# Dilated attention, then a binary convolution: group-norm statistics of two layers through one set of products

## The chip, the cores and the metric

The kernel runs on one core of one Trainium2 chip. The metric is device time in microseconds (us); the time of a kernel is the median of its runs. Profiles come from one profiled execution, whose own time is given beside its span. In the rows, PE is the matmul engine (TensorE), PEld its weight loads, DVE is VectorE, ACT is ScalarE, POOL is GpSimd and SP is the engine that issues most DMAs.

## The reference

The input `x` has 16 images of 56 x 56 pixels and 384 channels, in float32. Two layers follow each other, both with a group norm in front and a residual around them:

```python
def _gn(v, G=32, eps=1e-5):          # 32 groups of 12 channels, over a whole image
    g = v.reshape(B_, H_, W_, G, C_ // G)
    m = jnp.mean(g, axis=(1, 2, 4), keepdims=True)
    s = jnp.var(g, axis=(1, 2, 4), keepdims=True)
    return ((g - m) / jnp.sqrt(s + eps)).reshape(v.shape)

x = x + attention(_gn(x), w_qkv, w_proj, b_proj)   # layer 0
x = x + depthwise_conv3x3(_gn(x), sign(w))         # layer 1
```

The attention of layer 0 splits the channels into three sets of 128 with dilations 1, 2 and 3, each with four heads of 32 channels. Every pixel attends to its 3 x 3 neighbours at that dilation; a 384 x 384 projection with a bias follows. What matters here is that a group norm needs the mean and variance over the whole image before any pixel of it can be normalised.

## The kernel before

The work is cut into chunks of 8 rows (448 pixels): 7 chunks an image, 112 in all, numbered `m`; `b` is the image and `c` the chunk within it. Every tile has channels on the partitions, three tiles of 128.

Three stages run at once on different chunks.

- Stage A (`plan_a`) loads a chunk of `x` (L407), turns it with 12 TensorE transposes (L412), copies the three results out of PSUM on ScalarE (L424), takes their per-channel statistics on VectorE (`bn_stats`, L425) and stores them channel-first in DRAM as `xd` (L427, three stores). `xd` has three buffers, one image each. For image 0 it runs ahead of everything else.
- Stage B (`plan_b`) loads from `xd` (L455), normalises on ScalarE (L459), forms q, k and v on TensorE (L463), copies k and v out (L473) with halo rows exchanged by DMA (L477, L478), multiplies q by the shifted keys on VectorE (L516), sums over channels on TensorE (L501), takes the softmax, spreads the weights on TensorE (`pb_a`, L582), multiplies by the shifted values (L589), adds up on GpSimd (L597 to L601), projects (`po`, L615), adds the residual (L618), takes layer 1's statistics (L621) and stores `x1d` (L623).
- Stage C (`plan_c`) loads `x1d` (L694, L745), normalises (L713, L756), convolves two channel sets on TensorE (`pc`, L727) and the third on ScalarE and GpSimd (L778, L784 to L792), turns the result back (L799), copies it out (L801) and stores it.

The order of the work is a plan in slices. `at(when, order, piece)` puts a piece of work at slice `when`; nine slices make a step (`STEP = 9`), and chunk `m` of stage B starts at step `m`. All pieces are emitted in the order of slice and then of kind, and the framework makes each engine's in-order queue from that, by its own estimate of when things are ready:

```python
plan_a(m, STEP * (m - 9))
plan_b(m, STEP * m)
plan_c(m, STEP * (m + 10))
```

So before the change stage A of a chunk runs nine steps ahead of its stage B, and stage C ten steps behind.

The statistics of an image (`group_norm`) are a chain of six pieces, put at slices 0, 1, 2, 4, 5 and 7 from their start. `channels` merges the seven chunks' statistics per channel (`bn_aggr`, L305). `mean` sums channels into the 32 groups with three TensorE products (`pm`, L311). `deviation` sends the mean back to the channels (`pb`, L321) and squares the difference on GpSimd (L324, L325). `variance` sums again (`pv`, L331), `invert` takes the inverse root in 13 GpSimd operations (L345 to L349), and `spread_out` sends mean and scale to the channels (`pp`, L354, copied to `mr` at L358). For layer 1, 24 more small products (`pz`, L367) make a second copy, `mrz`, in stage C's layout. Each float32 product is two matmul instructions in the profile.

The chain runs 32 times: for layer 0 of image `b` from slice 5 of the step in which stage A has its last chunk (step 7b-3), and for layer 1 of image `b` from the start of step 7b+9. Within the seven steps of an image, numbered from 0, layer 1's chain therefore lies in the third step and layer 0's, for the image after next, in the fifth and sixth. Stage C's new image starts in the fourth.

The PSUM tiles of stage A, of k and v, of `po`, of `pc`, of the outputs and of the statistics all share one pool of three buffers, `ps_mt`.

Of the kernel before, what the change touches and what calls it, by code (L numbers as in the profile page):

```python
# [8 lines left out]
F32 = mybir.dt.float32  # L9
# [3 lines left out]
ALU = mybir.AluOpType  # L13
# [4 lines left out]
P = 128  # L18
HEADS = 4
HD = 32  # L20
NG = 3
NTAP = 9
NQ = 4
ROWS = 8
SUB = 112
GN_CH = 12
GN_G = 32
# [8 lines left out]
def dilated_attention_then_binary_conv(  # L36
# [28 lines left out]
    nc = tc.nc  # L65
    B, H, W, C = x.shape
    PX = ROWS * W
    NCH = H // ROWS
# [4 lines left out]
    K3 = 3 * HD  # L73
    JG = NG - 1
# [217 lines left out]
            for m in matmuls[1:]:  # L292
                tc.keep_in_program_order(m())

    def group_norm(stats, done, for_convolution=False):

        had = {}  # L300

        def channels():
            had["ch"] = ch = st_p.tile([P, NG, 2], F32, tag="ch", name="ch")
            for j in range(NG):
                nc.vector.bn_aggr(ch[:, j, :], stats[:, j].rearrange("p c s -> p (c s)"))  # L305

        def mean():
            had["pair"] = pair = st_p.tile([GN_G, 3], F32, tag="pair", name="pair")
            pm = ps_mt.tile([P, 512], F32, tag="mt", name="pm")
            for j in range(NG):  # L310
                nc.tensor.matmul(  # L311
                    pm[:GN_G, 0:1], gsel[:, j], had["ch"][:, j, 0:1], start=(j == 0), stop=(j == NG - 1)
                )
            nc.vector.tensor_scalar_mul(pair[:, 2:3], pm[:GN_G, 0:1], -1.0 / GN_CH)

        def deviation():

            ch = had["ch"]
            pb = ps_mt.tile([P, 512], F32, tag="mt", name="pb")
            for j in range(NG):  # L320
                nc.tensor.matmul(pb[:, j : j + 1], gselT[:, j], had["pair"][:, 2:3], start=True, stop=True)  # L321
            had["dev"] = dev = st_p.tile([P, NG], F32, tag="dev", name="dev")
            nc.vector.tensor_tensor(dev, pb[:, :NG], ch[:, :, 0], ALU.add)
            nc.gpsimd.tensor_tensor(dev, dev, dev, ALU.mult)  # L324
            nc.gpsimd.tensor_tensor(dev, dev, ch[:, :, 1], ALU.add)  # L325

        def variance():
            dev = had["dev"]
            pv = ps_mt.tile([P, 512], F32, tag="mt", name="pv")
            for j in range(NG):  # L330
                nc.tensor.matmul(pv[:GN_G, 0:1], gsel[:, j], dev[:, j : j + 1], start=(j == 0), stop=(j == NG - 1))  # L331
            had["var"] = var = st_p.tile([GN_G, 3], F32, tag="var", name="var")
            v, r = var[:, 0:1], var[:, 1:2]
            nc.vector.tensor_scalar(v, pv[:GN_G, 0:1], 1.0 / GN_CH, 1e-5, op0=ALU.mult, op1=ALU.add)

            ri = r.bitcast(I32)
            nc.vector.tensor_single_scalar(ri, v.bitcast(I32), 1, op=ALU.arith_shift_right)
            nc.vector.tensor_scalar(ri, ri, -1, RSQRT_BITS, op0=ALU.mult, op1=ALU.add)

        def invert():  # L340

            var, pair = had["var"], had["pair"]
            v, r, t = var[:, 0:1], var[:, 1:2], var[:, 2:3]
            for step in range(3):
                nc.gpsimd.tensor_tensor(t, r, r, ALU.mult)  # L345
                nc.gpsimd.tensor_tensor(t, t, v, ALU.mult)
                nc.gpsimd.tensor_scalar(t, t, -0.5, 1.5, op0=ALU.mult, op1=ALU.add)
                nc.gpsimd.tensor_tensor(pair[:, 1:2] if step == 2 else r, r, t, ALU.mult)
            nc.gpsimd.tensor_tensor(pair[:, 0:1], pair[:, 2:3], pair[:, 1:2], ALU.mult)  # L349

        def spread_out():
            pp = ps_mt.tile([P, 512], F32, tag="mt", name="pp")
            for j in range(NG):
                nc.tensor.matmul(  # L354
                    pp[:, 2 * j : 2 * j + 2], gselT[:, j], had["pair"][:, 0:2], start=True, stop=True
                )
            mr = st_p.tile([P, NG, 2], F32, tag="mr", name="mr", bufs=4)
            nc.vector.tensor_copy(mr.rearrange("p j s -> p (j s)"), pp[:, : 2 * NG])  # L358
            if not for_convolution:
                done(mr)  # L360
                return

            pz = ps_mt.tile([P, 512], F32, tag="mt", name="pz")
            for s in range(JG * NQ):
                of_set = gselT[:, s // NQ, s % NQ * HD : s % NQ * HD + HD]
                for ky in range(3):
                    nc.tensor.matmul(  # L367
                        pz[ky * HD : (ky + 1) * HD, 2 * s : 2 * s + 2], of_set, had["pair"][:, 0:2],
                        start=True, stop=True,
                    )  # L370
            mrz = st_p.tile([K3, JG, NQ, 2], F32, tag="mrz", name="mrz")
            nc.vector.tensor_copy(mrz.rearrange("p j q s -> p (j q s)"), pz[:K3, : 2 * JG * NQ])
            done(mr, mrz)

        return channels, mean, deviation, variance, invert, spread_out

# [5 lines left out]
    def at(when, order, piece):  # L382

        pieces.setdefault((when, order), []).append(piece)
# [6 lines left out]
    def plan_a(m, t0):  # L391

        b, c = divmod(m, NCH)
        had = {}

        def load():
            if c == 0:
                stats0[b] = st_p.tile([P, NG, NCH, 6], F32, tag="stats0", name="stats0")
                xd[b] = dr_p.tile([C, H * W], F32, tag="xd", name="xd")
            if b == 0 and c % 3:  # L400

                xin = z_p.tile([P, NQ * PX], F32, tag="z", name="xin_z")[:SUB, : NSUB * C]
                xin = xin.rearrange("p (s c) -> p s c", s=NSUB)
            else:
                xin = xin_p.tile([SUB, NSUB, C], F32, tag="xin", name="xin")
            had["xin"] = xin
            nc.sync.dma_start(xin, xf[b, c * PX : (c + 1) * PX, :].rearrange("(s p) c -> p s c", p=SUB))  # L407

        def turn(j):
            pt = ps_mt.tile([P, 512], F32, tag="mt", name="pt_x")  # L410
            for s in range(NSUB):
                nc.tensor.transpose(  # L412
                    pt[:, s * SUB : (s + 1) * SUB], had["xin"][:, s, j * P : (j + 1) * P], ident[:SUB, :SUB]
                )
            if b == 0:

                if j == 0:
                    pool, tag = ((xn_p, "xn"), (xn_p, "xn"), (xn_p, "xn"), (xr_p, "xr"), (t_p, "t"), (w_p, "w"),
                                 (w_p, "w"))[c]
                    first[c] = pool.tile([P, NG, PX], F32, tag=tag, name="x_first")  # L420
                xa = first[c][:, j]
            else:
                xa = xa_p.tile([P, PX], F32, tag="xa", name="xa")
            nc.scalar.copy(xa, pt[:, :PX])  # L424
            nc.vector.bn_stats(stats0[b][:, j, c, :], xa)  # L425
            if b:
# [4 lines left out]
        steps = {}  # L431

        def norm(k):
            if k == 0:
                steps["of"] = group_norm(stats0.pop(b), lambda mr: mr0.update({b: mr}))
            steps["of"][k]()

        at(t0 - 3 if b else FIRST + 2 * max(c - 2, 0), LOADS, load)
        for j in range(NG):
            at(t0 + 2 * j if b else FIRST + 2 * c + 1, STAGE_A, lambda j=j: turn(j))  # L440
        if c == NCH - 1:
            for k in range(6):
                at(t0 + 5 + STAT0_SLICE[k], STAT_ORDER[k], lambda k=k: norm(k))

    def plan_b(m, t0):

        b, c = divmod(m, NCH)
        had = {}
# [173 lines left out]
            if j == NG - 1:  # L622
                nc.sync.dma_start(chunk_of(x1d[b], c), xr)  # L623

        steps = {}

        def norm(k):
            if k == 0:
                steps["of"] = group_norm(stats1.pop(b), lambda mr, mrz: mr1.update({b: (mr, mrz)}), True)
            steps["of"][k]()  # L630
# [17 lines left out]
        at(t0 + 20, LOADS, load_residual)  # L648
        for j in range(NG):
            at(t0 + 24 + j, PROJECT, lambda j=j: out_project(j))  # L650
        if c == NCH - 1:
            for k in range(6):
                at(t0 + 27 + STAT1_SLICE[k], STAT_ORDER[k], lambda k=k: norm(k))

    def plan_c(m, t0):

# [181 lines left out]

    STAT_ORDER = (STATISTICS, SPREAD, SPREAD, SPREAD, STATISTICS, SPREAD)
    STEP = 9  # L840
    STAT0_SLICE = (0, 1, 2, 4, 5, 7)
    STAT1_SLICE = (0, 1, 2, 4, 5, 7)
    FIRST = -200
    at(FIRST, LOADS, load_weights)
    for cc in range(NG):
# [3 lines left out]
    for o in range(NTAP):  # L849
        at(-17 + o, LOADS, lambda o=o: load_taps(*divmod(o, 3)))  # L850
    at(5, LOADS, small_weights)
    for m in range(N):
        plan_a(m, STEP * (m - 9))
        plan_b(m, STEP * m)
        plan_c(m, STEP * (m + 10))
    for key in sorted(pieces):
# [30 lines left out]
```

## Time and profile before

| | us |
|---|---|
| median of 3 runs | 5411.35 |
| lowest and highest | 5409.35, 5414.15 |
| profiled execution, own time | 5406.89 |
| its span in the trace | 5405.2 |
| TensorE busy | 5205.9 |
| GpSimd busy | 4215.2 |
| VectorE busy | 4150.0 |
| ScalarE busy | 2397.8 |

The page gives busy times over the whole span. Since the work repeats every seven steps, the stretches of single steps say more than the averages; the prediction reads those. An answer for a line of the kernel gives how long its instructions were busy, the mean of one in ns, and how long its engine idled just before them and what ended that.

### The profile page before, as it was taken

The page shows a single profiled execution, that of the slowest core. Times are in us where ns is not written, and L with a number is a line of the kernel's source. Part 1 is how long each engine was busy: PE and PEld are TensorE (multiplying, and loading weights), DVE is VectorE, ACT ScalarE, POOL GpSimd, SP SyncE. Part 2 cuts the span into 40 slices and gives each one's busy share as a digit, 9 for nine tenths or more (in the row PEclk, how much of TensorE's full clock was granted, in tenths as well). Part 3 has the DMA queues.
Part 4 walks back from the last instruction along what each step waited for, and adds up shares of the span by engine and source line. Part 5 has one row for each costly group of instructions (what it writes and reads, how often), then busy time and mean ns, then how long its engine had stood idle before and what let it go on. Part 6 is the DMA issues. An engine that isn't in the chain of part 4 may idle for free. (4 is left out here: it accounts for less than half of the span.)

```text
span 5405.2 us, 77297 instructions
## 1 busy us (share of the span) xinstructions
PE 5205.9 (96%) x27669; PEld 2414.4 (45%) x27669; DVE 4150.0 (77%) x4209; ACT 2397.8 (44%) x4189; POOL 4215.2 (78%) x3049
## 2 busy tenths in 40 slices
PE   8999999999999999999999999999999999999965
PEld 4444444444444444444444444444444444444422
DVE  4887777878777787777777777787777778777754
ACT  3224444444444444444444444444444444444433
POOL 2677888888888887888888788888888888888880
PEclk9999999999999999999999999999999999999976
DMA  5444555655555555555655655555555655544443
GB/s 168 127 120 124 159 157 158 163 154 161 158 158 160 164 159 159 157 157 158 163 154 161 164 152 160 164 157 163 159 157 154 164 154 161 161 130 134 122 130 126
DMA packets 810799, 825.73 MB, mean 153 GB/s; under 512 B 359467, under 2 KB 800174, under 8 KB 810414
## 3 DMA queue, kind: packets, MB, share of 16 engines
q1 hardware_dynamic: 802430, 808.79, 54.2%
q10 hardware_dynamic: 7984, 12.00, 0.7%
q8 instruction: 219, 3.59, 0.3%
q14 instruction: 166, 1.36, 0.1%
HBM read 466.41 MB, written 231.21 MB: 129 GB/s over the span
## 5 line engine op out<-in xcount | busy, mean ns | idle before, releaser
L597 POOL TENSOR_TENSOR w<-w 128x1344 f32<-128x1344 f32 x672 | 2049.9, 3050 | 456.2 <-DVE w L589 396.7
L589 DVE TENSOR_TENSOR w<-pb_a,v 128x1344 f32<-128x1344 f32 x1008 | 1559.1, 1547 | 267.0 <-PE pb_a L582 177.4
L516 DVE TENSOR_TENSOR t<-pq,k 128x1344 f32<-128x1344 f32 x1008 | 1535.8, 1549 | 237.0 <-PE pq L463 236.1
L463 PE MATMUL pkv<-xn,wqkvT 128*128 128x448 f32 x3924 | 1569.9, 549 | 9.0 <-ACT xa L424 4.7
L463 PEld LDWEIGHTS pkv<-xn,wqkvT 128*128 128x128 f32 x3924 | 718.4, 190 | 671.8 <-issue 629.4
L615 PE MATMUL po<-y,wprojT 128*128 128x448 f32 x2016 | 834.9, 550 | 27.4 <-POOL y L601 15.0
L784 POOL TENSOR_TENSOR m<-m 128x1344 f32<-128x1344 f32 x210 | 644.7, 3070 | 274.1 <-ACT m L778 274.0
L463 PE MATMUL pq<-xn,wqkvT 128*128 128x448 f32 x1962 | 830.7, 558 | 0.0
L713 ACT ACTIVATE z<-z,mrz 96x448 f32<-96x448 f32 x840 | 578.3, 751 | 350.9 <-DMA z<-x1d 330.3
L501 PE MATMUL ps<-t,sel 128*32 128x448 f32 x6048 | 666.0, 550 | 26.0 <-DVE t L516 25.3
L778 ACT ACTIVATE m<-zg,ktap 128x448 f32<-128x448 f32 x945 | 555.5, 658 | 274.0 <-POOL m L784 266.9
L615 PEld LDWEIGHTS po<-y,wprojT 128*128 128x128 f32 x2016 | 376.4, 191 | 382.9 <-issue 341.1
L727 PE MATMUL pc<-z,kdiag 96*32 96x440 f32 (+1 forms) x5040 | 516.7, 543 | 6.4 <-POOL z L715 4.6
L463 PEld LDWEIGHTS pq<-xn,wqkvT 128*128 128x128 f32 x1962 | 344.0, 189 | 316.9 <-issue 316.9
L734 DVE TENSOR_TENSOR x<-pc,x 128x448 f32<-128x448 f32 x224 | 139.3, 622 | 353.2 <-PE pc L727 342.1
L582 PE MATMUL pb_a<-aT,spread 24*128 24x448 bf16 x3024 | 369.1, 359 | 32.2 <-DVE w L589 25.9
L601 POOL TENSOR_TENSOR y<-y,w 128x448 f32<-128x448 f32 x336 | 381.5, 1135 | 22.6
L618 DVE SCALAR_TENSOR_TENSOR xr<-po,bias,xr 128x448 f32<-128x448 f32 x336 | 227.5, 677 | 220.9 <-PE po L615 217.2
L600 POOL TENSOR_TENSOR y<-w 128x448 f32<-128x448 f32 x336 | 382.2, 1138 | 14.7
L473 ACT COPY v<-pkv 128x448 f32<-128x448 f32 x336 | 178.3, 531 | 484.1 <-PE pkv L463 475.8
L473 ACT COPY k<-pkv 128x448 f32<-128x448 f32 x336 | 178.2, 530 | 376.5 <-PE pkv L463 376.5
L501 PEld LDWEIGHTS ps<-t,sel 128*32 128x32 f32 x6048 | 170.6, 110 | 364.9 <-issue 247.8
(131 smaller groups left out, 4394.7 us busy)
## 6 DMA issues: line engine op xcount, KB each, us to landing
z<-x1d SPq DMA_DIRECT2D x570, 224.0 KB
xr<-xd SPq DMA_DIRECT2D x112, 672.0 KB
x1d<-xr SPq DMA_DIRECT2D x112, 672.0 KB
xn<-xd SPq DMA_DIRECT2D x109, 672.0 KB
xin<-in_x_dram SPq DMA_DIRECT2D x108, 672.0 KB
xd<-xa SPq DMA_DIRECT2D x315, 224.0 KB
out_dram<-osb SPq DMA_DIRECT2D x420, 168.0 KB
x<-x1d SPq DMA_DIRECT2D x112, 448.0 KB
```

The costliest lines, as they stand in the source:

```text
L463: nc.tensor.matmul(dst[:, :PX], wqkvT[:, cc, o0 : o0 + P], had["xn"][:, cc, :], start=(cc == 0), stop=(cc == NG - 1))
L501: return nc.tensor.matmul(had["ps"][32 * j : 32 * j + 32, :PX], sel[:, s0 : s0 + 32], tk, start=(issued[j] == 1), stop=(issued[j] == len(r ...
L516: nc.vector.tensor_tensor(t.rearrange("p k (r w) -> p k r w", w=W), q3, k3, ALU.mult)
L589: nc.vector.tensor_tensor(w.rearrange("p k (r w) -> p k r w", w=W), pb[:, :, :PX].rearrange("p k (r w) -> p k r w", w=W), three(kv[1][g][m ...
L597: nc.gpsimd.tensor_tensor(w0, w0, w, ALU.add)
L600: nc.gpsimd.tensor_tensor(y, w0[:, 0], w0[:, 1], ALU.add)
L601: nc.gpsimd.tensor_tensor(y, y, w0[:, 2], ALU.add)
L615: nc.tensor.matmul(po[:, :PX], wprojT[:, g, j * P : (j + 1) * P], had[f"y{g}"], start=(g == 0), stop=(g == NG - 1))
L713: nc.scalar.activation(z, z, AF.Identity, bias=mrz[:, j, q, 0:1], scale=mrz[:, j, q, 1:2])
L727: return nc.tensor.matmul(pcr[q * HD : (q + 1) * HD, :, lo:hi], kdiag[:, kx, j * NQ + q, :], rows(set_of(j, q))[:, :, lo + kx - 1 : hi + k ...
L778: nc.scalar.activation(rows(t[:, kx]), zp[:, ky : ky + ROWS, kx : kx + W], AF.Copy, scale=ktap[:, o : o + 1])
L784: nc.gpsimd.tensor_tensor(had["m"], had["m"], t, ALU.add)
```

## The change

Stage A is moved from nine steps ahead to twelve. As that can't be done before the kernel starts, chunks 7 to 9 stay where they were, and chunks 10, 12 and 14 are slipped in one slice later within steps 0, 1 and 2, beside the chunk that runs there anyway; they load into buffers (`z_p`) that stage C uses only later. From chunk 15 on, a chunk starts exactly three steps earlier than before.

With that, the last chunk of image b+2 is through stage A in step 7b+8, just before layer 1's statistics of image `b` at step 7b+9. `group_norm` now takes a list of sets and carries them side by side as columns: `ch`, `pair`, `dev`, `var` and `mr` get a dimension `L`, the products `pm`, `pb` and `pv` have `L` columns and `pp` has `2L`, and the small vector operations work on `L` columns at once. The aggregates (three for each set) and the products `pz` (for layer 1 only) stay one for each set. The statistics of layer 0 of images 0 and 1 run alone, as do those of layer 1 of images 14 and 15; the other 14 pairs run together, in layer 1's place.

```diff
-    def group_norm(stats, done, for_convolution=False):
+    def group_norm(sets):
         had = {}
+        L = len(sets)
 
         def channels():
-            had["ch"] = ch = st_p.tile([P, NG, 2], F32, tag="ch", name="ch")
-            for j in range(NG):
-                nc.vector.bn_aggr(ch[:, j, :], stats[:, j].rearrange("p c s -> p (c s)"))
+            had["ch"] = ch = st_p.tile([P, L, NG, 2], F32, tag=f"ch{L}", name="ch")
+            for n, (stats, _, _) in enumerate(sets):
+                for j in range(NG):
+                    nc.vector.bn_aggr(ch[:, n, j, :], stats[:, j].rearrange("p c s -> p (c s)"))
...
-                    pm[:GN_G, 0:1], gsel[:, j], had["ch"][:, j, 0:1], start=(j == 0), stop=(j == NG - 1)
+                    pm[:GN_G, 0:L], gsel[:, j], had["ch"][:, :, j, 0], start=(j == 0), stop=(j == NG - 1)
...
-                nc.tensor.matmul(pb[:, j : j + 1], gselT[:, j], had["pair"][:, 2:3], start=True, stop=True)
+                nc.tensor.matmul(
+                    pb[:, j * L : (j + 1) * L], gselT[:, j], had["pair"][:, :, 2], start=True, stop=True
+                )
...
-                nc.tensor.matmul(pv[:GN_G, 0:1], gsel[:, j], dev[:, j : j + 1], start=(j == 0), stop=(j == NG - 1))
+                nc.tensor.matmul(pv[:GN_G, 0:L], gsel[:, j], dev[:, :, j], start=(j == 0), stop=(j == NG - 1))
...
-                    pp[:, 2 * j : 2 * j + 2], gselT[:, j], had["pair"][:, 0:2], start=True, stop=True
+                    pp[:, 2 * L * j : 2 * L * (j + 1)], gselT[:, j], pair[:, :, 0:2], start=True, stop=True
...
-            if b == 0 and c % 3:
+            if (b == 0 and c % 3) or m in doubled:
...
-        if c == NCH - 1:
-            for k in range(6):
-                at(t0 + 5 + STAT0_SLICE[k], STAT_ORDER[k], lambda k=k: norm(k))
...
-        if c == NCH - 1:
-            for k in range(6):
-                at(t0 + 27 + STAT1_SLICE[k], STAT_ORDER[k], lambda k=k: norm(k))
...
+    AHEAD = 12
+    doubled = (10, 12, 14)
+
+    def start_a(m):
+        behind = max(m - AHEAD, -2 + m - NCH - len([d for d in doubled if d <= m]))
+        return STEP * (behind if m >= NCH else m - 9) + (m in doubled)
...
+    for b in range(2):
+        statistics(start_a(NCH * b + NCH - 1) + 5, [(0, b)])
+    for b in range(B):
+        last = NCH * b + NCH - 1
+        statistics(STEP * last + 27, [(1, b)] + ([(0, b + 2)] if b + 2 < B else []))
     for m in range(N):
-        plan_a(m, STEP * (m - 9))
+        plan_a(m, start_a(m))
```

More of the change, by code (lines that the diff above doesn't have):

```diff
@@ L293, in in_one_go @@
                 tc.keep_in_program_order(m())
-    def group_norm(stats, done, for_convolution=False):
+    def group_norm(sets):
         had = {}
+        L = len(sets)
         def channels():
-            had["ch"] = ch = st_p.tile([P, NG, 2], F32, tag="ch", name="ch")
-            for j in range(NG):
-                nc.vector.bn_aggr(ch[:, j, :], stats[:, j].rearrange("p c s -> p (c s)"))
+            had["ch"] = ch = st_p.tile([P, L, NG, 2], F32, tag=f"ch{L}", name="ch")
+            for n, (stats, _, _) in enumerate(sets):
+                for j in range(NG):
+                    nc.vector.bn_aggr(ch[:, n, j, :], stats[:, j].rearrange("p c s -> p (c s)"))
         def mean():
-            had["pair"] = pair = st_p.tile([GN_G, 3], F32, tag="pair", name="pair")
+            had["pair"] = pair = st_p.tile([GN_G, L, 3], F32, tag=f"pair{L}", name="pair")
             pm = ps_mt.tile([P, 512], F32, tag="mt", name="pm")
@@ L311, in mean @@
                 nc.tensor.matmul(
-                    pm[:GN_G, 0:1], gsel[:, j], had["ch"][:, j, 0:1], start=(j == 0), stop=(j == NG - 1)
+                    pm[:GN_G, 0:L], gsel[:, j], had["ch"][:, :, j, 0], start=(j == 0), stop=(j == NG - 1)
                 )
-            nc.vector.tensor_scalar_mul(pair[:, 2:3], pm[:GN_G, 0:1], -1.0 / GN_CH)
+            nc.vector.tensor_scalar_mul(pair[:, :, 2], pm[:GN_G, 0:L], -1.0 / GN_CH)
         def deviation():
@@ L320, in deviation @@
             for j in range(NG):
-                nc.tensor.matmul(pb[:, j : j + 1], gselT[:, j], had["pair"][:, 2:3], start=True, stop=True)
-            had["dev"] = dev = st_p.tile([P, NG], F32, tag="dev", name="dev")
-            nc.vector.tensor_tensor(dev, pb[:, :NG], ch[:, :, 0], ALU.add)
+                nc.tensor.matmul(
+                    pb[:, j * L : (j + 1) * L], gselT[:, j], had["pair"][:, :, 2], start=True, stop=True
+                )
+            had["dev"] = dev = st_p.tile([P, L, NG], F32, tag=f"dev{L}", name="dev")
+            nc.vector.tensor_tensor(
+                dev, pb[:, : NG * L].rearrange("p (j l) -> p l j", l=L), ch[:, :, :, 0], ALU.add
+            )
             nc.gpsimd.tensor_tensor(dev, dev, dev, ALU.mult)
-            nc.gpsimd.tensor_tensor(dev, dev, ch[:, :, 1], ALU.add)
+            nc.gpsimd.tensor_tensor(dev, dev, ch[:, :, :, 1], ALU.add)
         def variance():
@@ L330, in variance @@
             for j in range(NG):
[L331 to L334, printed above, removed]
+                nc.tensor.matmul(pv[:GN_G, 0:L], gsel[:, j], dev[:, :, j], start=(j == 0), stop=(j == NG - 1))
+            had["var"] = var = st_p.tile([GN_G, 3, L], F32, tag=f"var{L}", name="var")
+            v, r = var[:, 0], var[:, 1]
+            nc.vector.tensor_scalar(v, pv[:GN_G, 0:L], 1.0 / GN_CH, 1e-5, op0=ALU.mult, op1=ALU.add)
             ri = r.bitcast(I32)
@@ L342, in invert @@
             var, pair = had["var"], had["pair"]
-            v, r, t = var[:, 0:1], var[:, 1:2], var[:, 2:3]
+            v, r, t = var[:, 0], var[:, 1], var[:, 2]
             for step in range(3):
@@ L347, in invert @@
                 nc.gpsimd.tensor_scalar(t, t, -0.5, 1.5, op0=ALU.mult, op1=ALU.add)
-                nc.gpsimd.tensor_tensor(pair[:, 1:2] if step == 2 else r, r, t, ALU.mult)
-            nc.gpsimd.tensor_tensor(pair[:, 0:1], pair[:, 2:3], pair[:, 1:2], ALU.mult)
+                nc.gpsimd.tensor_tensor(pair[:, :, 1] if step == 2 else r, r, t, ALU.mult)
+            nc.gpsimd.tensor_tensor(pair[:, :, 0], pair[:, :, 2], pair[:, :, 1], ALU.mult)
         def spread_out():
+            pair = had["pair"]
             pp = ps_mt.tile([P, 512], F32, tag="mt", name="pp")
@@ L354, in spread_out @@
                 nc.tensor.matmul(
-                    pp[:, 2 * j : 2 * j + 2], gselT[:, j], had["pair"][:, 0:2], start=True, stop=True
+                    pp[:, 2 * L * j : 2 * L * (j + 1)], gselT[:, j], pair[:, :, 0:2], start=True, stop=True
                 )
[L357 to L373, printed above, removed]
+            mr = st_p.tile([P, NG, L, 2], F32, tag=f"mr{L}", name="mr", bufs=5 - L)
+            nc.vector.tensor_copy(mr.rearrange("p j l s -> p (j l s)"), pp[:, : 2 * L * NG])
+            for n, (_, done, for_convolution) in enumerate(sets):
+                if not for_convolution:
+                    done(mr[:, :, n])
+                    continue
+                pz = ps_mt.tile([P, 512], F32, tag="mt", name="pz")
+                for s in range(JG * NQ):
+                    of_set = gselT[:, s // NQ, s % NQ * HD : s % NQ * HD + HD]
+                    for ky in range(3):
+                        nc.tensor.matmul(
+                            pz[ky * HD : (ky + 1) * HD, 2 * s : 2 * s + 2], of_set, pair[:, n, 0:2],
+                            start=True, stop=True,
+                        )
+                mrz = st_p.tile([K3, JG, NQ, 2], F32, tag="mrz", name="mrz")
+                nc.vector.tensor_copy(mrz.rearrange("p j q s -> p (j q s)"), pz[:K3, : 2 * JG * NQ])
+                done(mr[:, :, n], mrz)
         return channels, mean, deviation, variance, invert, spread_out
@@ L429, in turn @@
                 nc.scalar.dma_start(chunk_of(xd[b], c), first[c])
[L431 to L436, printed above, removed]
         at(t0 - 3 if b else FIRST + 2 * max(c - 2, 0), LOADS, load)
@@ L623, in out_project @@
                 nc.sync.dma_start(chunk_of(x1d[b], c), xr)
[L625 to L630, printed above, removed]
         at(t0 - 18, LOADS, load_x)
@@ L840, in dilated_attention_then_binary_conv @@
     STEP = 9
-    STAT0_SLICE = (0, 1, 2, 4, 5, 7)
-    STAT1_SLICE = (0, 1, 2, 4, 5, 7)
+    STAT_SLICE = (0, 1, 2, 4, 5, 7)
     FIRST = -200
@@ L851, in dilated_attention_then_binary_conv, with statistics, norm @@
     at(5, LOADS, small_weights)
+    AHEAD = 12
[3 more added lines that the diff above has]
+        return STEP * (behind if m >= NCH else m - 9) + (m in doubled)
+    def statistics(when, sets):
+        steps = {}
+        def norm(k):
+            if k == 0:
+                steps["of"] = group_norm([
+                    (stats1.pop(b), lambda mr, mrz, b=b: mr1.update({b: (mr, mrz)}), True) if layer
+                    else (stats0.pop(b), lambda mr, b=b: mr0.update({b: mr}), False)
+                    for layer, b in sets
+                ])
+            steps["of"][k]()
+        for k in range(6):
+            at(when + STAT_SLICE[k], STAT_ORDER[k], lambda k=k: norm(k))
+    for b in range(2):
[3 more added lines that the diff above has]
+        statistics(STEP * last + 27, [(1, b)] + ([(0, b + 2)] if b + 2 < B else []))
     for m in range(N):
-        plan_a(m, STEP * (m - 9))
+        plan_a(m, start_a(m))
         plan_b(m, STEP * m)
```

## The prediction

> **What bounds the kernel now.** I read the page's busy shares first, then busy time by step, then TensorE's timeline in the steps that are long, then the list of waits. A step is the 9 slices of one chunk; I took its ends from the starts of each chunk's first score product (L516) in the timeline. Seven steps make an image.
>
> ```profile
> PE 5205.9 (96%) x27669; PEld 2414.4 (45%) x27669; DVE 4150.0 (77%) x4209; ACT 2397.8 (44%) x4189; POOL 4215.2 (78%) x3049
> PEclk9999999999999999999999999999999999999976
> ```
>
> TensorE is the fullest engine by far, at full clock. The windows show what that means for one step (columns: window, length, then busy us and instructions of PE, PEld, DVE, ACT, POOL, clock, DMA share, GB/s):
>
> ```profile
> 2310.50:2355.40 44.90, 44.90 (x235) 20.69 (x234) 36.47 (x36) 22.63 (x40) 38.01 (x23) 1.00 0.63 168
> 2355.40:2403.00 47.60, 47.60 (x306) 23.19 (x306) 36.82 (x43) 16.33 (x30) 36.61 (x37) 1.00 0.59 156
> 2403.00:2450.00 47.00, 45.58 (x234) 20.53 (x233) 36.53 (x34) 26.93 (x49) 39.06 (x20) 1.00 0.59 159
> 2450.00:2496.90 46.90, 45.87 (x247) 21.70 (x246) 37.63 (x40) 21.53 (x38) 39.78 (x26) 1.00 0.58 160
> 2496.90:2543.50 46.60, 45.72 (x246) 21.67 (x245) 36.32 (x38) 23.15 (x41) 38.95 (x40) 1.00 0.55 156
> 2543.50:2588.40 44.90, 44.90 (x234) 20.67 (x234) 35.91 (x34) 20.51 (x37) 37.46 (x23) 1.00 0.58 156
> ```
>
> A plain step is 44.9 us and TensorE is busy in all of it. The second row carries layer 1's statistics (72 more matmuls, no idle time), the third the start of a new image in stage C, and the fourth and fifth layer 0's statistics: 12 more matmuls each, and each about 1.8 us longer. Before stage C runs, the same two steps are 40.5 against 39.5 us (252.5 to 293.0 against 293.0 to 332.5), so the extra belongs to the statistics. What it consists of:
>
> ```profile
> 2487.41 0.72 PE L321 MATMUL pb<-pair,gselT 32*128 32x1 f32 x6
> 2489.16 2.52 PE L615 MATMUL po<-y,wprojT 128*128 128x448 f32 x6 [1.03 <-ACT k L473]
> ...
> 2501.12 0.35 PE L331 MATMUL pv<-dev,gsel 128*32 128x1 f32 x6 [0.88 <-POOL dev L325]
> ```
> ```profile
> PE pv L331 <- POOL dev L325: 10.8, 13, 0.9
> PE po L615 <- ACT k L473: 9.7, 10, 1.4
> ACT zg L756 <- DVE mr L358: 74.1, 16, 8.8
> ```
>
> The 13 waits of `pv` and the 10 of `po` all lie in layer 0's statistics of images 2 to 15. `pv` stands at the head of TensorE's queue until GpSimd has squared the deviations. `po` waits because `pb` took one of the three `ps_mt` buffers, so the buffer it gets is the one ScalarE has still to empty. The third row matters below: layer 1's result is already late for ScalarE.
>
> **The change, part by part.**
>
> *Removed.* For images 2 to 15, 14 times, layer 0's products lose their own pass: 24 matmuls (12 products, two passes each), 6 small VectorE operations (`pair`, `dev`, three of `var`, `mr`), 15 GpSimd operations and four `ps_mt` buffers. TensorE's time, by the windows: 45.87 - 44.90 = 0.97 and 45.72 - 44.90 = 0.82, together 1.8 us an image; 14 x 1.8 = 25.2. The waits go too: 10.8 + 9.7 = 20.5. VectorE's 6 x 0.14 = 0.8 us and GpSimd's 15 x 0.19 = 2.9 us an image lie under TensorE (VectorE idles about 9 us of such a step, GpSimd about 7) and count as nothing; without that cover they would be a further gain. Sum: -45.7.
>
> Two rules of the Trainium skill speak for less. The windows show that identical TensorE work takes 44.9 us again and again with no idle time; "Perfetto Trace Analysis", section "Identifying the Most-Contended Engine", says that matmul busy time is no measure of how near the engine is to its limit, and to read the weight-load share instead, here 45%. By it TensorE has room and only the 20.5 us of waits would go. I follow the windows: 12 added matmuls lengthen the step even where nothing waits (40.5 against 39.5). And the measured 1.8 us for 24 matmuls is 75 ns each; "TensorE: Matmul & The Clock Gate", section "Back-to-back issue gap", gives a floor of about 25 ns for such a narrow one, 0.6 us a set, 8.4 us in all, and a sum of 28.9 instead of 45.7. The trace has the duration, so 75 ns stands.
>
> *Widened.* Layer 1's products now have two columns, or four in `pp`. The trace has one- and two-column products:
>
> ```profile
> L321 PE MATMUL pb<-pair,gselT 32*128 32x1 f32 x192 | 26.0, 247 | 0.3 <-DVE pair L314 0.3
> L354 PE MATMUL pp<-pair,gselT 32*128 32x2 f32 x192 | 24.7, 241 | 2.4 <-POOL pair L349 2.4
> L305 DVE BATCH_NORM_AGGREGATE ch<-stats 128x2 f32<-128x42 f32 x96 | 31.9, 335 | 1.5
> ```
>
> A second column costs nothing there: 0. No row shows one whose columns lie apart in memory, as they do now; if that doubled the products' cost it would be 1.8 us x 14 = 25, if anything is saved it is noise. I take 0, by the nearest row. The small vector operations likewise.
>
> *Moved on VectorE.* Layer 0's three aggregates, 3 x 0.335 = 1.0 us, now stand ahead of `pm` in the first statistics step. Behind them in VectorE's queue are the weighing products that free `pb_a`; VectorE idles 10.8 us of that step. In the traced image the last aggregate ends at 2360.8 and `pm` starts at 2364.5; further on, `pair` is ready at 2389.5 and `pp` starts at 2394.0. So 1.0 us is covered by 3.6 and again by 4.6 us: 0. Without the cover it is up to 1.0 x 14 = 14 us, since ScalarE waits for `mr` (74.1 us in 16 waits).
>
> *Moved in stage A.* From chunk 15 on it runs three steps earlier at the same slices; chunks 10, 12 and 14 are added to steps 0, 1 and 2, and steps 100 to 102 have none. Each chunk brings one load (L407) and three stores (L427) on SP, 12 transposes, three ScalarE copies and three `bn_stats`. TensorE's part:
>
> ```profile
> L412 PE MATMUL pt_x<-ident,xin 112*128 112x112 f32 x1296 | 187.4, 269 | 12.7 <-DMA xin<-in_x_dram 12.7
> ```
> ```profile
> 4765.60:4811.00 45.40, 44.52 (x234) 20.50 (x234) 34.80 (x36) 21.04 (x37) 37.81 (x39) 1.00 0.46 129
> 4811.00:4855.20 44.20, 43.72 (x222) 19.48 (x221) 34.49 (x32) 18.55 (x33) 36.40 (x23) 1.00 0.45 120
> ```
>
> 187.4 / 108 = 1.7 us a chunk of busy time; the last row has no stage A and is 44.2, so 0.7 us comes back per step at the end, where other waits fill in. Steps 0 to 2 have TensorE busy in 28.10 of 28.1, 30.15 of 31.6 and 37.15 of 38.6 us, so most of it is paid there: 3 x 1.4 - 3 x 0.7 = +2. ScalarE (7 to 9 us busy) and VectorE (15 to 33) have room; chunks 10, 12 and 14 load into a buffer that stage C doesn't use before step 9. Image 1's own statistics move from steps 4 and 5 to 2 and 3 at the same price: 0. On SP the 12 extra issues, at about 0.45 us each, pass the halo copies (L477, L478) that the score products wait for; a store whose `xa` isn't copied yet holds SP (58.8 us in 46 waits over the whole run, 9.5 at most). That bounds this part from above at about +20 for three steps; from below it is -2, if every waiting moment is filled. I take +2. In the steady state SP gets the same issues in each step; the `xd` buffer that image b+3 reuses is last read one step before it is first written instead of four, about 40 us apart, so no wait. POOL issues nothing in stage A.
>
> *Sum:* -45.7 + 2 = -43.7. The profiled execution took 5406.89 us (span 5405.2 and 1.7 around it), 4.5 less than the median of 5411.35; from the median: 5368.
>
> **The rivals.**
>
> *The freed time turns into another wait.* In the third window above TensorE already idles 1.4 us, where GpSimd's additions hold VectorE and that holds `pb_a` and `ps`; GpSimd is at 39.8 of 46.9 us in the next, and would be at 39.4 of 44.9. If 1.4 us an image came back: 14 x 1.4 = 20, time 5388. Against it: the steps after show no such wait, and GpSimd loses 2.9 us of work an image. If instead only waits were saved, as the first rule has it: 5411 - 20.5 + 2 = 5393.
>
> *Slower: the joint chain comes a slice late.* ScalarE waits 4.6 us an image for `mr`, and behind that wait are the copies which empty TensorE's PSUM tiles; how a late ScalarE reaches TensorE shows once, in the first image, where TensorE idles 4.73 us at 477.35 before `pkv` until ScalarE has copied `xa`. If the order of work put one joint product a slice (5.0 us) later, 14 x 5.0 = 70 would be lost against 43.7 won: 5438. It decides from 43.7 / 14 = 3.1 us of lateness an image after the slack of 3.6 and 4.6. Against it: the added work is 1.0 us.
>
> *Less comes together than meant.* Image b+2's last stage A product is at slice 9(7b+8)+4, the joint pass starts at 9(7b+9), five slices later; so all 14 pair up and this is out.
>
> *More is gained.* Six of the 14 images also show a wait of 1.46 us of `ps` for VectorE early in the fourth step, some with a lower clock after it. With less GpSimd work these may go: about -16, time 5352.
>
> **How the numbers follow.** The sum as worked out, 5355 to 5378: 0.60. Part of it back as waits, matmul time hidden or columns dear, 5380 to 5398: 0.24. More gained: 0.06. Nothing that can be told: 0.05. Slower: 0.05. About 0.2% (11 us) is what a measurement of this kernel can tell from none. Range 5352 to 5392, cut inside the second case; faster 0.90, within 0.05, slower 0.05.
>
> **What would show it.** After: L311, L321, L331 and L354 with 108 matmuls each instead of 192; the fourth and fifth steps of an image at 44.9 to 45.3 us; no wait of `pv` on GpSimd; the first statistics step still 47.6 with no TensorE idle; ScalarE's wait for `mr` near 74 us; steps 0 to 2 longer by some 4 us together. A fourth step that stays near 46 with a new wait makes the first rival right; a longer wait for `mr` with TensorE idle behind it, the slower one.

## The result, and the profile after

| | before | after |
|---|---|---|
| median, us | 5411.3 (4 runs, 5409.35 to 5414.15) | 5360.56 (4 runs, 5358.26 to 5362.08) |
| ratio, 95% interval | | 0.9905 [0.9888, 0.9923] |
| profiled execution, us | 5406.89 | 5362.08 |
| mean of an image's seven steps, steps 11 to 101, us | 324.0 | 320.4 |

The change makes the kernel 50.7 us faster by the medians and 44.8 us by the profiled executions. The page's first part, with the same columns as before:

```profile
PE 5174.7 (97%) x27333; PEld 2385.0 (44%) x27333; DVE 4189.1 (78%) x4125; ACT 2400.3 (45%) x4189; POOL 4178.0 (78%) x2839
```

TensorE has 336 instructions fewer, 14 sets of 24, and 31.2 us less work. GpSimd has 210 fewer, 14 sets of 15. The groups of instructions (line, engine, operation, tiles, shapes, count; busy us, mean ns; idle before) show the 14 joint passes with their two and four columns (`pv` and `pm` have 84 of their own too):

```profile
L325 PE MATMUL pb<-pair,gselT 32*128 32x2 f32 x84 | 11.6, 250 | 0.0
L363 PE MATMUL pp<-pair,gselT 32*128 32x4 f32 x84 | 10.1, 234 | 0.0
```

84 = 14 x 6. A `pb` matmul of two columns that lie apart takes 250 ns; one of one column took 247. The windows below, in the columns of before (window, length, busy us and instructions of PE, PEld, DVE, ACT, POOL, clock, DMA share, GB/s), are the third to sixth steps of an image, and then the fifth of an earlier image:

```profile
2341.50:2389.00 47.50, 47.50 (x306) 23.13 (x305) 39.30 (x42) 16.49 (x30) 36.66 (x37) 1.00 0.56 156
2389.00:2436.10 47.10, 45.71 (x235) 20.59 (x234) 36.57 (x35) 26.59 (x48) 37.94 (x19) 1.00 0.59 159
2436.10:2482.20 46.10, 44.92 (x234) 20.66 (x233) 36.68 (x35) 18.92 (x34) 37.27 (x24) 1.00 0.54 146
2482.20:2528.00 45.80, 44.97 (x234) 20.65 (x233) 36.78 (x35) 26.43 (x46) 38.92 (x28) 1.00 0.62 175
833.70:878.50 44.80, 44.80 (x234) 20.63 (x233) 36.68 (x34) 19.65 (x35) 37.65 (x23) 1.00 0.57 152
```

The third step carries both sets now and is as long as before, 47.5 us without idle time. The fifth and sixth have lost their 12 matmuls each: TensorE is busy 44.9 to 45.0 us in both, where it was 45.7 to 45.9. In the earlier image nothing else is left and the fifth step is a plain one, as is its sixth. In the other image 1.18 and 0.83 us of idle time remain; the timeline puts both on `ps`, which waits for VectorE's product. In the fifth steps that wait was there before; in the sixth it is new. In the list of waits (us, times, longest), the first row of before, the others of after:

```profile
PE ps L501 <- DVE t L516: 25.3, 34, 1.7
```
```profile
PE ps L501 <- DVE t L516: 28.0, 41, 1.7
PE po L615 <- ACT k L473: 1.7, 1, 1.7
ACT zg L746 <- DVE mr L367: 73.6, 16, 8.8
```

`pv` no longer waits for GpSimd at all, and the 10 waits of `po` for `k` are gone; the one in the list is new, in step 2, where image 1's own chain now runs. By the position in the image, as means over steps 11 to 101 with TensorE's idle time in brackets, in us:

| | third | fourth | fifth | sixth |
|---|---|---|---|---|
| before | 47.57 (0) | 47.23 (1.59) | 47.99 (1.50) | 46.55 (0.76) |
| after | 47.47 (0.01) | 47.15 (1.51) | 46.09 (0.75) | 45.02 (0.11) |

The other three are equal within 0.03. An image gains 3.57 us. In the fifth and sixth steps 1.40 of it is idle time and 2.03 TensorE's own time. The 0.10 of the third come from step 100, which no longer has a chunk of stage A.

### The profile page after: what moved, and what is told of

The parts are those of the page before. It is cut to its first block, busy times and chain, and to the rows that moved or that the text cites. A ratio compares the mean times of both kernels' runs of the same rounds, so it can differ in the third digit from the quotient of the medians.

```text
span 5360.3 us, 76299 instructions
## 1 busy us (share of the span) xinstructions
PE 5174.7 (97%) x27333; PEld 2385.0 (44%) x27333; DVE 4189.1 (78%) x4125; ACT 2400.3 (45%) x4189; POOL 4178.0 (78%) x2839
## 4 chain that ended last, share of the span: by engine, by line
PE 77%; POOL 7%; DVE 7%; DMA 4%; ACT 2%; issue 1%; SPq 1%; POOLq 0%; ACTq 0%; DVEq 0%
PE pkv L463 23%; PE pq L463 13%; PE po L615 11%; PE ps L501 10%; PE pc L717 8%; PE pb_a L582 5%; POOL w L597 3%; DVE t L516 3%; DVE w L589 2%; PE pt_x L422 2%; PE pt_o L789 2%; POOL m L774 2%; PE pt_s L536 1%; ACT m L768 1%; DMA z_last<-x1d 1%
## 5 line engine op out<-in xcount | busy, mean ns | idle before, releaser
L774 POOL TENSOR_TENSOR m<-m 128x1344 f32<-128x1344 f32 x210 | 644.5, 3069 | 281.7 <-ACT m L768 281.5
```

Of the source, the lines that this page charges most:

```text
L774: nc.gpsimd.tensor_tensor(had["m"], had["m"], t, ALU.add)
```

## The experiments

The theory was that of the prediction: what pays is that layer 0's products and their waits vanish, because as second columns they cost nothing; moving stage A is only what makes it possible. The rivals were that stage A's new place pays by itself, that the new place of layer 0's chain pays, and not the joining, and that the waits alone are the gain. All kernels were timed in five rounds beside the kernel before, whose medians there were 5410.5 to 5411.6. Diffs are against the changed kernel unless said otherwise.

**Stage A ahead, chains where they were.**

```diff
-    for b in range(2):
-        statistics(start_a(NCH * b + NCH - 1) + 5, [(0, b)])
+    for b in range(B):
+        statistics(STEP * (NCH * b + NCH - 1 - 9) + 5, [(0, b)])
...
-        statistics(STEP * last + 27, [(1, b)] + ([(0, b + 2)] if b + 2 < B else []))
+        statistics(STEP * last + 27, [(1, b)])
```

> Stage A three steps ahead as in the changed kernel, but every layer 0 chain runs alone, in the slices it had before the change. Theory A (the gain is layer 0's own pass leaving TensorE): no gain, 5408 to 5418 us, with the waits of pv on GpSimd and of po on ScalarE back at about 20 us and 192 matmuls each of pm, pb, pv and pp. Theory B (the gain comes from stage A being early: a shorter end, another pattern of transfers): under 5390 us.

Measured: 5413.6 us, ratio 1.0008 [1.0, 1.0017]. Moving stage A gains nothing, and costs 3 us by the medians and 9 at most by the interval, as the first theory had it. The waits are back with the chains:

```profile
PE pv L339 <- POOL dev L333: 12.6, 12, 2.9
PE po L615 <- ACT k L473: 11.8, 12, 2.0
```

**Both chains in the same slices, each with its own products.**

```diff
-        statistics(STEP * last + 27, [(1, b)] + ([(0, b + 2)] if b + 2 < B else []))
+        statistics(STEP * last + 27, [(1, b)])
+        if b + 2 < B:
+            statistics(STEP * last + 27, [(0, b + 2)])
```

> Layer 0's chain of image b+2 is put into the same slices as layer 1's of image b, but with products, PSUM tiles and small operations of its own. Theory A (24 matmuls take 1.8 us of TensorE a set wherever they stand): 5361 + 14 x 1.8 = 5386 us if no wait comes with them, up to 5405 if the PSUM tiles of two chains make new waits. Theory C (narrow matmuls are hidden in the pipeline, only waits were saved): 5361 to 5368 us.

Measured: 5441.34 us, 1.0058 [1.0046, 1.0071]: slower than before, 80.8 us over the changed kernel and above both forecasts. The place alone doesn't pay. The third and fourth steps of one image in the windows, then the list of waits:

```profile
2366.70:2416.60 49.90, 49.45 (x330) 24.93 (x329) 37.10 (x49) 16.52 (x30) 38.69 (x52) 1.00 0.55 149
2416.60:2466.20 49.60, 47.02 (x234) 21.28 (x233) 38.93 (x34) 27.29 (x49) 38.32 (x20) 0.97 0.55 151
```
```profile
PE pb_a L582 <- DVE w L589: 48.8, 22, 4.7
```

The 24 matmuls (330 against 306) make TensorE busy 49.45 - 47.50 = 1.95 us longer, in a step where it barely waits. So 14 x 1.8 to 1.95 = 25 to 27 us of the 80.8 is the products themselves. The rest is new and has two parts.

The first is a wait: in the fourth step `pb_a` waits 2.58 us for VectorE, and the clock falls to 0.97 over that step. The timeline (start us, us, instruction, count, and idle before it in brackets) of this kernel, and then one row of the changed kernel:

```profile
2426.28 3.03 POOL L774 TENSOR_TENSOR m<-m 128x1344 f32<-128x1344 f32 x1
2426.45 3.34 DVE L549 TENSOR_TENSOR ew<-ew,sm 112x432 f32<-112x432 f32 x1
2431.31 0.37 PE L582 MATMUL pb_a<-aT,spread 24*128 24x448 bf16 x3 [2.58 <-DVE w L589]
```
```profile
2398.36 0.91 DVE L549 TENSOR_TENSOR ew<-ew,sm 112x432 f32<-112x432 f32 x1
```

The softmax's product on VectorE (L549) takes 3.34 us where it took 0.91. It starts just behind an addition of GpSimd (L774) and ends 0.47 us after that has ended, and the product that `pb_a` needs stands behind it in VectorE's queue. In 12 of the 13 images of steps 11 to 101 it takes 3.34 to 3.37 us there, and each ends 0.47 us after GpSimd's instruction; in the changed kernel it is long in one image only. So the moved pieces made two instructions meet that do not meet in the changed kernel.

The second is the clock. In nine third steps of this stretch it falls to half behind the small products, with at most 0.33 us of idle time in the 3.41 us before. The windows on either side of such a fall, in an earlier image:

```profile
776.70:780.11 3.41, 3.41 (x70) 2.52 (x72) 2.37 (x3) 0.00 (x0) 0.27 (x2) 1.00 0.47 82
780.11:783.52 3.41, 3.41 (x22) 0.84 (x14) 0.52 (x4) 0.81 (x1) 3.33 (x2) 0.50 0.54 201
```

Over steps 11 to 101 the profiled execution is 68.4 us longer than the changed kernel's: TensorE idles 18.2 us more and is busy 50.2 us more. It runs at half clock for 75 us instead of 14, which is up to 61 / 2 = 31 us of the 50.2.

**The chain left out.** On the kernel before, layer 0's chain is left out for images 2 to 15, which take image 1's mean and scale instead; so the output of those images isn't the reference's.

```diff
...
+        def other_norm():
+            stats0.pop(b)
+            mr0[b] = mr0[1]
...
-            for k in range(6):
+            for k in range(6 if b < 2 else 0):
                 at(t0 + 5 + STAT0_SLICE[k], STAT_ORDER[k], lambda k=k: norm(k))
+            if b >= 2:
+                at(t0 + 5, STATISTICS, other_norm)
```

> The kernel before with the layer 0 chain of images 2 to 15 left out; they are normalised with image 1's mean and scale, so this times the kernel without those chains. Theory A (a second column costs nothing, the whole price of the chain is what left the fifth and sixth step): 45 us less than before, 5366 us, within 6 us of the changed kernel. Theory D (columns and aggregates in the joint chain have a price of their own): 5340 to 5350 us, well below the changed kernel.

Measured: 5359.34 us, 0.9904 [0.9891, 0.9918], against 5360.56 and 0.9905 of the changed kernel. The whole of 14 chains was worth 51 us, and the joining gets all of it: the second column, the three more aggregates, and stage A's move together cost nothing that shows in the time. The third step of an image:

```profile
2332.10:2379.60 47.50, 47.50 (x306) 23.15 (x305) 36.79 (x42) 17.13 (x32) 36.73 (x37) 1.00 0.60 160
```

The third step is 47.50 us here without layer 0's columns and 47.50 in the changed kernel with them. VectorE is busy 36.79 against 39.30 us, which TensorE doesn't see.

**The joint chain a slice later.**

```diff
-        statistics(STEP * last + 27, [(1, b)] + ([(0, b + 2)] if b + 2 < B else []))
+        statistics(STEP * last + 28, [(1, b)] + ([(0, b + 2)] if b + 2 < B else []))
```

> The changed kernel with layer 1's chain, joint or alone, put one slice (5 us) later. The slower rival of the prediction says that every microsecond of lateness of mr beyond the slack reaches TensorE: 16 x 5 = 80 us, 5440 us. Theory A as I hold it (ScalarE already waits 4.6 us an image for mr while TensorE idles only 1.4 us in the step after): some of it is covered, 5375 to 5405 us, with ScalarE's wait for mr near 150 us. If the chain is not near TensorE's path at all: 5361 us.

Measured: 5390.36 us, 0.9960 [0.9948, 0.9973]. In steps 11 to 101 a slice of lateness costs 27.7 us, 27.7 / 13 = 2.1 an image. The time lies where the theory had it, but ScalarE's wait for `mr`, which was to be near 150 us and which the slower rival was to be read from, fell:

```profile
ACT zg L746 <- DVE mr L367: 46.0, 16, 11.0
```

**The joint chain's second half sooner.** `variance`, `invert` and `spread_out` a slice sooner; in the second kernel the last of them two.

```diff
-    STAT_SLICE = (0, 1, 2, 4, 5, 7)
+    STAT_SLICE = (0, 1, 2, 3, 4, 6)   # the second kernel: (0, 1, 2, 3, 4, 5)
```

> The changed kernel with the last three pieces of every statistics chain one slice (5 us) sooner (slices 0, 1, 2, 3, 4, 6). A slice later cost 30 us, 2 us an image, in the steps where stage C starts an image. Theory E (mr sets when stage C's first work lands, and sooner is better): 5335 to 5350 us, the fourth step of an image below 46.5. Theory F (the later cost came from new collisions of the moved products, not from mr): about 5361 us, or more if pv and pp now wait for GpSimd (slack 4.2 and 4.6 us against a slice of 5.0).

> As the run before, with the last piece two slices sooner (slices 0, 1, 2, 3, 4, 5). Theory E: another 10 to 15 us less than that run, as long as GpSimd's 13 operations are done in time. Theory F: TensorE waits for pair at pp, 2 to 4 us an image, 5390 to 5410 us.

Measured: 5371.47 us, 0.9931 [0.9918, 0.9943], and 5386.55 us, 0.9950 [0.9936, 0.9964]. Both are slower than the changed kernel, so theory E's times are missed, and what theory F said of `pv` came true. In the first, the fourth and fifth steps gain 1.4 us together (46.48 and 45.32 against 47.15 and 46.09), but the third is 49.52 instead of 47.47, because `variance` now comes before GpSimd has squared:

```profile
PE pv L339 <- POOL dev L333: 22.4, 15, 3.9
```

The second has that wait too (22.5 us), but the wait of `pp` for GpSimd that theory F named did not come (0.2 us in all). Instead `pb_a` waits 1.5 us for VectorE in the fourth step of 12 images, behind an L549 of 2.5 us that again ends 0.47 us after an instruction of GpSimd.

**Image 1's own chain put back** to steps 4 and 5.

```diff
-    for b in range(2):
-        statistics(start_a(NCH * b + NCH - 1) + 5, [(0, b)])
+    statistics(STEP * -3 + 5, [(0, 0)])
+    statistics(STEP * 4 + 5, [(0, 1)])
```

> The changed kernel with layer 0's chain of image 1 back in steps 4 and 5, where it was before the change, instead of steps 2 and 3. In the changed kernel's trace steps 2 to 5 together are 4.0 us longer than before, beyond the moved transposes: pb takes a PSUM buffer in step 2 and po waits 1.74 us there with a lower clock after it. If that is the cause: steps 2 to 5 shorter by 3 to 5 us, 5356 us. If it is only that step 2 has more to do: no change, 5361 us.

Measured: 5356.95 us (5356.3 to 5362.3), 0.9905 [0.9891, 0.9918]. By the medians this is 3.6 us under the changed kernel, but the ratios are the same, so the times don't tell the two apart. The steps do: steps 2 to 5 take 39.45, 39.46, 40.47 and 40.51 us, and in the changed kernel 43.77, 40.52, 39.45 and 39.45. The difference is 3.3 us, and most of it is one wait in step 2 of the changed kernel, first in the timeline and then in the windows:

```profile
169.44 0.72 PE L325 MATMUL pb<-pair,gselT 32*128 32x1 f32 x6
171.90 4.01 PE L615 MATMUL po<-y,wprojT 128*128 128x448 f32 x6 [1.74 <-ACT k L473]
```
```profile
172.00:175.90 3.90, 3.90 (x10) 1.66 (x14) 0.09 (x2) 0.00 (x0) 3.90 (x4) 0.62 0.04 8
```

`po` waits 1.74 us right behind `pb`, and then takes 4.01 us for what took 2.52, at a clock of 0.62.

**Layer 0's own pass, re-timed.** Two kernels on the kernel before, to see whether its waits can be had without joining: the pieces from `deviation` to `invert` a slice later, or `variance` and what follows it.

```diff
-    STAT0_SLICE = (0, 1, 2, 4, 5, 7)
+    STAT0_SLICE = (0, 1, 3, 5, 6, 7)   # the second kernel: (0, 1, 2, 5, 6, 8)
```

> The kernel before, with layer 0's chain in the same two steps but its later pieces one slice later (slices 0, 1, 3, 5, 6, 7), so that pv no longer stands right behind GpSimd's additions and pb stands at another place. Theory A (25 us of the gain were TensorE time and 20 us were waits bound to these places): the waits of pv and po go, 5385 to 5395 us. If the waits merely move on with the chain: 5405 to 5415 us. If TensorE time were not the price, all of the gain: 5366 us.

> The kernel before, with the last three pieces of layer 0's chain one slice later (slices 0, 1, 2, 5, 6, 8), the gap between GpSimd's inverse root and pp unchanged. Theory A: only the 13 waits of pv on GpSimd go, 11 us: 5400 us; the waits of po, which belong to pb, and TensorE's time stay. If the wait of pv was no loss because TensorE would have waited elsewhere: 5408 to 5412 us.

Measured: 5502.09 us, 1.0170 [1.0156, 1.0184], far above every forecast, and 5403.79 us, 0.9988 [0.9982, 0.9995]. In the first the waits of `pv` for GpSimd and of `po` for `k` went, but `spread_out` stood one slice behind `invert` instead of two, and TensorE waited for its result:

```profile
PE pp L354 <- POOL pair L349: 71.9, 16, 7.1
```

In the second, which lies between its two forecasts, `pv` no longer waited either, and `po` did so more, 18.1 us where it was 9.7:

```profile
PE po L615 <- ACT k L473: 18.1, 13, 2.7
```

So of the 51 us these two re-timings had 7.8 at best (5403.8 against 5411.6 beside it; 10 at most by the interval).

**Only the last piece sooner**, with image 1's chain put back as above.

```diff
-    STAT_SLICE = (0, 1, 2, 4, 5, 7)
+    STAT_SLICE = (0, 1, 2, 4, 5, 6)
```

> The changed kernel with layer 0's chain of image 1 back in steps 4 and 5 (as in the earlier run with that alone, 5357 us) and only the last piece of each chain one slice sooner (slices 0, 1, 2, 4, 5, 6), so that pv stays where it is. Moving pv as well made the fourth and fifth steps of an image 1.4 us shorter and the third 2.1 us longer, with pv waiting for GpSimd. If the first came from mr being sooner and the second from pv alone: 5357 - 15 x 1.4 = 5336 us. If GpSimd isn't done with its 13 operations by then (slack 4.6 us against 5.0) pp waits and the lower clock that followed such waits comes with it: 5365 to 5400 us.

Measured: 5447.4 us, 1.0068 [1.0055, 1.008], 90 us over the kernel with only image 1's chain put back and above both forecasts. The third step is 53.53 us, 2.98 of it idle. The list of waits, the timeline and the windows of one image:

```profile
PE pp L363 <- POOL pair L357: 45.3, 15, 3.6
```
```profile
2413.51 1.44 PE L363 MATMUL pp<-pair,gselT 32*128 32x4 f32 x6 [2.94 <-POOL pair L357]
2415.82 4.55 PE L463 MATMUL pkv<-xn,wqkvT 128*128 128x448 f32 x6
2420.60 2.52 PE L463 MATMUL pkv<-xn,wqkvT 128*128 128x448 f32 x6
```
```profile
2413.50:2417.00 3.50, 3.50 (x56) 3.05 (x57) 1.22 (x3) 0.81 (x1) 2.93 (x1) 0.50 0.21 47
2417.00:2420.50 3.50, 3.50 (x8) 1.18 (x7) 0.59 (x1) 0.09 (x1) 0.00 (x0) 0.58 0.00 0
```

A wait of 2.94 us is followed by 7 us at a clock of 0.50 and 0.58; six matmuls of `pkv` take 4.55 us there and 2.52 right after. The waits of `pp` are 45 us, and those of `pb_a` for VectorE are 12 us more than without the edit (38.7 against 26.6): in the fourth step of 12 images L549 takes 2.6 to 2.7 us and ends behind GpSimd once more. Other waits shrank. Over steps 11 to 101 TensorE idles 37.7 us more and is busy 52.7 us more with the same instructions; it runs at half clock for 119 us instead of 7, so the clock cost more than the waits.

## Why the prediction was right

*The base.* The sum was -43.7 from one profiled execution to the other; it was -44.8. The forecast of 5368 is 7.4 above the median because the execution before was 4.5 under its median and the one after is 1.5 over its own. That the sum came within 1.1 is partly luck: the joining brought 2.7 more than forecast, and the start and the end together cost 1.5 more.

*The removed products and waits, -45.7.* Steps 11 to 101 hold 13 of the 14 joint passes and went from 4212.0 to 4165.7 us: -46.3, where 13 x 3.26 = 42.4 was forecast. Steps 102 and 103, the place of the fourteenth, became 2.1 shorter. The stretch varies by some us with the waits in it: with stage A ahead and the chains in their old places it took 4205.1. Leaving the chains out altogether gives the same time as joining them, and giving the products back in the joint slices lengthens TensorE's busy time by 1.95 us a set, which the prediction had at 1.8. The extra 0.3 us an image is the clock, and largely luck: in the fifth steps of this stretch it fell to half five times before and three times after, 3.41 us each, and 2 x 1.7 / 13 = 0.26. One of the five stood behind a wait of `po` that is gone, the other four behind waits of `ps`, which both kernels have. What is left of the 2.03 us of TensorE's own time is 1.77, the products at 74 ns a matmul. Both rules that spoke for less fell to this. The weight-load share of 45% did not mean that TensorE could hide 24 more matmuls; the section names the share of peak arithmetic beside it, which was not worked out. And each matmul cost about 74 to 81 ns, not 25. But the section on the issue gap says itself that its figures for single matmuls are too low for small ones that come with a weight load each, and has 81 ns for 128 columns in such a stream; the prediction took the floor without that.

*The columns, 0.* 250 ns against 247 for `pb`; shown again by the equal third steps with and without them.

*The aggregates, 1.0 us covered.* The cover held: no idle time, and ScalarE's wait for `mr` was 73.6 us against 74.1. The size was off: VectorE's busy time in that step grew by 2.5 us in the windows (36.82 to 39.30).

*Stage A's move, +2.* Timed alone it cost 3 us, 9 at most, which fits. The step that failed in size is image 1's own chain, "at the same price: 0": it cost 3.3 in steps 2 and 3. Until step 11 the kernel lost 8.1 us (506.6 to 514.7). Beside those 3.3, the added chunks cost 2.4 in steps 0 to 2, where 4.2 was forecast; 0.6 lies in step 9, with the first joint pass; and 1.8 lies ahead of step 0, where the kernels run here differ by as much with the same plan (74.2 to 76.0). At the end, from step 102 on, 686.6 became 679.9. Of these 6.7, 2.1 are steps 102 and 103, 1.7 are steps 104 to 110, and 2.9 lie in the stretch from step 111 on, which takes 270 to 277 us over the kernels run here without a cause that was found. Of steps 100 and 101, which lost a chunk, one became 1.3 shorter and the other 1.6 longer. So the 2.1 that the missing chunks were to give back can't be told from the rest.

*The rivals.* The prediction counts the rows of its windows, so what it calls the fourth and fifth steps are the fifth and sixth here. The freed time did not turn into another wait: the fifth step waits 0.67 us for `ps` on average, and before it waited 0.69; new are only 0.11 us in the sixth. The forecast of 44.9 to 45.3 us for the fifth overlooked that wait: the mean is 46.09. "More is gained" had those waits go, and they didn't; up to step 102 a 1.46 us wait of `ps` shows in the fifth step of 6 images before, of 5 after, of 6 with the chain left out, and of 1 to 12 in the other kernels. The slower rival had 5.0 us for a slice of lateness and wanted 3.1 to decide; a slice cost 2.1, so even a slice late the change is ahead (5390 against 5411). It also named the wrong sign: ScalarE's wait for `mr` fell in the late kernel and is no measure of that loss.

*Open.* That VectorE's L549 is held by GpSimd's instruction is read from its end, in four kernels; no kernel was run that keeps the two apart, and why other instructions of VectorE run beside GpSimd's at their usual length was not looked into. And that `po` waits because `pb` has taken a buffer rests on its place, right behind `pb`, and on its going and coming with the chain in four kernels; a pool with one more buffer was not tried.

## What to carry to other kernels

Small float32 products on a full TensorE cost their instructions, not their columns (two and four here): if two chains of them can be made to meet in the same products, the second is free, and leaving it out first tells what that is worth. To make them meet, a cheap stage was moved by three steps, which by itself brought nothing; so a change that enables another should be timed alone as well. In a plan of in-order queues, pieces moved by a slice or two cost 0.8 to 6.5 us an image in five kernels, sooner as well as later, and gained 0.6 in one (medians over 14 images). The cost lay in waits that the moved pieces set up, of TensorE for GpSimd or for VectorE, and in the clock behind them, so the products were joined in the slots that the one chain already had.

## What the runs showed of the hardware

TensorE's clock fell already after waits of about 1.5 us. After 2.94 us it was 0.50 and 0.58 for 7 us (above); after 1.74 us it was 0.62 for 3.9 us (above, in the head of the changed kernel). In the kernel before, a wait of 1.46 us of `ps` does the same, here in the windows around its end and from the fall of the clock on:

```profile
1160.00:1162.00 2.00, 0.54 (x6) 0.30 (x3) 2.00 (x3) 0.68 (x2) 2.00 (x2) 1.00 1.05 393
1162.45:1165.86 3.41, 3.41 (x24) 0.97 (x20) 3.23 (x4) 0.62 (x1) 2.26 (x4) 0.50 0.27 85
```

In steps 11 to 101 of all twelve kernels each fall went to half the clock and lasted 3.41 us or two or three times that; the 0.58 and 0.62 are such stretches averaged with full clock. Not every wait brings it: of the six waits of 1.46 us in fifth steps before, four did, and so did one of 1.18. The wait of 1.03 us that the prediction shows has no such tail: `po` behind it takes its usual 2.52 us. And with both chains side by side it came behind small products with next to no wait. The Trainium skill, "TensorE: Matmul & The Clock Gate", section "Part 1: The HAM clock gate (the "warmup" mystery)", puts the half clock behind an idle window of about 3.4 us. The length of the falls agrees with that figure, but here an idle time of half of it and less has brought one. The measurement decides: in this kernel a wait of 1.5 us or more can cost well over its length (37.7 us more idle time became 90.4 us in the kernel with only the last piece sooner), and a sum that counts only its length is too low.
